# Full attention of a four-block model: maxima as pairs of 64-row products, and the values' products one step later

## The chip, the cores and the metric

The kernel runs on one core of a Trainium2 chip. The metric is the device time of one execution in microseconds (us); of several executions the median is given. The engines are named as the profile names them: PE (TensorE's matrix products) with PEld (its weight loads), DVE (VectorE), ACT (ScalarE), POOL (GpSimd) and SP (SyncE, which here issues the DMAs).

## The reference

The model takes x of 4 batches, 1024 places and 128 channels through four blocks, each x + s * silu(f), with s an attention-like layer and f a feed-forward-like one. The change is in the attention of the third block (number 2), with 16 heads of 8 channels and no mask:

```python
x_norm = layer_norm(x, g1, beta1)
q = (x_norm @ Wq + bq).reshape(B, S, H, hd).transpose(0, 2, 1, 3)
k = (x_norm @ Wk + bk).reshape(B, S, H, hd).transpose(0, 2, 1, 3)
v = (x_norm @ Wv + bv).reshape(B, S, H, hd).transpose(0, 2, 1, 3)
q = apply_rope(q)
k = apply_rope(k)
q = q * (1.0 / jnp.sqrt(jnp.float32(hd)))
scores = jnp.einsum('bhqd,bhkd->bhqk', q, k)
attn = jax.nn.softmax(scores, axis=-1)
out = jnp.einsum('bhqk,bhkd->bhqd', attn, v)
```

Everything is float32. Blocks 0 and 1 have attentions of the same size with a window of 250 places and with a causal mask; the same function of the kernel, `_attention`, does all three, with `mode` "window", "causal" or "full".

## The kernel before

**Products of parts.** Scores are wanted in float32 precision from bfloat16 products. `_split` cuts q and k into three bfloat16 parts each, whose sum is the float32 number. A head has 8 channels, so all nine products of a part of q with a part of k fit into one product with 72 rows of contraction: tile `q9` holds in rows 24r to 24r+23 the three parts of q, for r = 0, 1, 2, and `k9` holds in the same rows the r-th part of k three times. Rows 72 to 74 of `k9` are ones; there `q9` takes the negative maximum of each query's scores, again in three parts, so that the score product itself subtracts the maximum. The rows above are zero against one.

**Units.** A unit is one batch and a group of four heads; there are 16 (`order`). For each:

- `load(n)` (L278) fills a pair `q9`, `k9` from DRAM with three DMAs for q and nine for k, and one that clears rows 72 to 74 of `q9` where an earlier unit left maxima. There are three pairs, used in turn.
- `maxima(n)` (L293) makes 32 steps. A step (`tile_of`) makes the scores of 128 queries of one head against all 1024 keys: two products into the two banks of a `max_ps` tile (PSUM, two such tiles), then one DVE reduction (L344) to the negative maximum. Two ending steps: `split` cuts the maxima into parts on POOL, `spread` turns them with PE and writes them with three DMAs (L371) into rows 72 to 74 of `q9`.
- `attend(n)` (L397) goes through 16 blocks (two halves of 512 queries, eight tiles of 128 keys). In a block, `weights` makes for each of the four heads the scores of 128 keys against 512 queries (tile `sc`, one of three PSUM banks) and their exponential on ACT (L417) into `pt`, a tile for two heads out of five buffers; `values` multiplies the weights with the values, the four heads side by side in four tiles of 32 columns of the array, and adds up over the eight blocks of a half in `o_ps`. Those products are float32 (two records each in the profile).

**Order.** The order on PE is the order of the program (`keep_in_program_order`); on the other engines and SP a scheduler orders what is ready. `rest` (L524) runs for each unit n the list `ahead` (20 steps of the maxima of unit n+1, `split`, then 12 steps of unit n+2 with `spread` of unit n+1 among the last) against the list `weights`, one step of each in turn (`_interleave`). In `weights` each block has two steps: `first` makes the scores of heads 0 and 1, `second` the values of the block before (`lag` is 1 for "full") and then the scores of heads 2 and 3. So PE's order in a block is: maxima, scores, maxima, values, scores. Other layers' steps are spread over the units as further lists (`plan`): the projections of the next batch, the second block's router and experts, a feed-forward layer, whose hidden tiles `h2` come from the five `pt` buffers too, and the ends of the block. Before the first unit, `begin` projects batch 0, issues `load(0)` and `load(1)` and makes all maxima of unit 0 and 12 steps of unit 1, among the products of the first router's experts. `load(n+2)` is issued at the start of unit n.

The line in `attend` that the change moves:

```python
            def second(hn=hn, i=i):
                if i >= lag:
                    values(*blks[i - lag])
                pair.pop(hn)(1)
```

Of the kernel before, what the change touches and what calls it, by code (L numbers as in the profile page):

```python
# [22 lines left out]
F32 = mybir.dt.float32  # L23
BF16 = mybir.dt.bfloat16
AF = mybir.ActivationFunctionType
ALU = mybir.AluOpType
AX = mybir.AxisListType
PSUM = bass.MemoryType.PSUM

P = 128  # L30
B, T, C = 4, 1024, 128
NT = T // P
# [57 lines left out]
def _ps1(k, name, shape=(P, 512), dtype=F32):  # L90

    return k.ps.tile(list(shape), dtype, tag="s", name=name, bufs=3)


def _ps2(k, name):

    return k.ps.tile([P, 2, 512], F32, tag="m", name=name, bufs=2)
# [88 lines left out]
def _attention(k, pool, mode, xT, w, out, rope=None):  # L186
# [7 lines left out]

    nc = k.nc
    scale = HD**-0.5
    dense = {}
    units = {}  # L200
    place = 16 * ("window", "causal", "full").index(mode)

    ps1, ps2 = (lambda name: _ps1(k, name)), (lambda name: _ps2(k, name))
    matmul, transpose = (lambda *args, **kw: _mm(k, *args, **kw)), (lambda *args: _tr(k, *args))
# [73 lines left out]
    def load(n):  # L278

        b, g = order[n]  # L280
        q9, k9 = k.q9[(place + n) % 3], k.k9[(place + n) % 3]
        heads = slice(4 * g, 4 * g + 4)
        for r in range(3):
            rows = slice(24 * r, 24 * r + 24)
            nc.sync.dma_start(q9[rows], dense["q", b][:, heads, :])
            of = dense["k", b][8 * r : 8 * r + 8, heads, :].unsqueeze(0).to_broadcast([3, 8, 4, T])
            for s in range(3):
                nc.sync.dma_start(k9[24 * r + 8 * s : 24 * r + 8 * s + 8], of[s])
        if place + n > 2:
            nc.sync.dma_start(q9[72:75].rearrange("p h t -> p (h t)"), k.zeros)  # L290
        units[n] = (q9, k9)

    def maxima(n):  # L293

        held = {}

        def tile_of(parts):


            def step():  # L300
                q9, k9 = units[n]
                if "neg" not in held:
                    held["neg"] = pool.tile([P, 4, NT], F32, tag="neg", name="neg", bufs=3)
                neg = held["neg"]
                ps = ps2("max_ps")
                flat = ps.rearrange("p a c -> p (a c)")
                _, qt0, _ = parts[0]
                lo = max(0, qt0 - 2) * P if mode == "window" else 0
                hi = T if mode == "full" else (qt0 + 1) * P
                width = hi - lo  # L310
                for j, qt, place in parts:
                    lhs = q9[:, j, qt * P : qt * P + P]
                    for c0 in range(lo, hi, 512):
                        c1 = min(c0 + 512, hi)
                        at = place + c0 - lo
                        masked = mode != "full" and c1 == hi
                        matmul(
                            flat[:, at : at + c1 - c0],
                            lhsT=lhs,
                            rhs=k9[:, j, c0:c1],  # L320
                            start=True,
                            stop=not masked,
                            skip_group_check=True,
                        )
                        if masked:
                            mw = min(c1 - c0, k.mask[mode].shape[1])

                            W = k.mask[mode].shape[1]
                            spans = [(W - P, W)]
                            if W - mw < W - CONTEXT:  # L330
                                spans.insert(0, (W - mw, W - CONTEXT))
                            for m0, m1 in spans:
                                matmul(
                                    flat[:, at + c1 - c0 - W + m0 : at + c1 - c0 - W + m1],
                                    lhsT=k.ident16,
                                    rhs=k.mask[mode][:, m0:m1],
                                    start=False,
                                    stop=m1 == W,
                                    skip_group_check=True,
                                )  # L340
                j0, m = parts[0][0], len(parts)
                stride = parts[1][2] - parts[0][2] if m > 1 else width
                of = flat[:, 0 : m * stride].rearrange("p (n c) -> p n c", n=m)[:, :, 0:width]
                nc.vector.tensor_reduce(neg[:, j0 : j0 + m, qt0], of, AX.X, ALU.max, negate=True)  # L344

            return step

        steps = []
        for qt in range(NT):
            width = T if mode == "full" else min((qt + 1) * P, 3 * P if mode == "window" else T)  # L350

            pitch = 128 if width == 128 else 256 if width == 256 else 512 if width <= 512 else 1024
            per = min(4, 1024 // pitch)
            for j in range(0, 4, per):
                steps.append(tile_of([(j + i, qt, i * pitch) for i in range(per)]))

        def split():
            neg = held.pop("neg")
            held["p"] = parts = pool.tile([P, 3, 4 * NT], BF16, tag="negp", name="negp", bufs=2)
            tmp = pool.tile([P, 4 * NT], F32, tag="negt", name="negt", bufs=2)  # L360
            _split(nc, nc.gpsimd, neg.rearrange("p j t -> p (j t)"), parts, tmp)

        def spread():
            q9, parts = units[n][0], held.pop("p")
            tp = _ps1(k, "neg_ps", (12 * NT, P), BF16)
            transpose(tp, parts.rearrange("p s c -> p (s c)"), k.ident16)
            rows = pool.tile([12 * NT, P], BF16, tag="negr", name="negr", bufs=2)
            nc.vector.tensor_copy(rows, tp)
            for s in range(3):
                to = q9[72 + s : 73 + s].rearrange("o j (t q) -> o (j t) q", t=NT)  # L370
                nc.sync.dma_start(to, rows[4 * NT * s : 4 * NT * s + 4 * NT, :])  # L371

        return steps, [split, spread]


    blocks = [[], []]
    lag = 1 if mode == "full" else 2
    for hf in range(2):
        for kt in range(NT):
            c0 = max(512 * hf, 0 if mode == "full" else kt * P)  # L380
            c1 = min(512 * hf + 512, (kt + 3) * P if mode == "window" else T)
# [15 lines left out]
    def attend(n):  # L397
        b, g = order[n]
        q9, k9 = units.pop(n)
        va = dense["va", b]  # L400
        held = {}
# [66 lines left out]
        blks = [(hf, i) for hf in range(2) for i in range(len(blocks[hf]))]  # L468
        steps = []
        pair = {}  # L470
        for i, hn in enumerate(blks):

            def first(hn=hn):
                pair[hn] = weights(*hn)
                pair[hn](0)

            def second(hn=hn, i=i):
                if i >= lag:
                    values(*blks[i - lag])
                pair.pop(hn)(1)  # L480
                if i > lag and blks[i - lag - 1][0] < blks[i - lag][0]:
                    normalize(0)

            steps += [first, second]
# [31 lines left out]
    order = [(b, g) for b in range(B) for g in range(4)]  # L516
    N = len(order)
    steps, ending = maxima(0)
    begin = project(0) + [lambda: load(0), lambda: load(1)] + steps + ending
    steps, ending = maxima(1)  # L520
    lead = 2 * len(steps) // 5
    begin += steps[:lead]
# [1 line left out]
    def rest(plan):  # L524

        nonlocal steps, ending
        late = []
        for n, (b, g) in enumerate(order):
            ahead = []
            if n + 1 < N:  # L530

                ahead = steps[lead:] + ending[:1]
                last = ending[1]
                if n + 2 < N:
                    load(n + 2)
                    steps, ending = maxima(n + 2)
                    ahead += steps[: lead - 2] + [last] + steps[lead - 2 : lead]
                else:
                    ahead.append(last)
            weights, closing = attend(n)  # L540
            streams = [ahead, weights]
            if b + 1 < B and g < 3:
                if g == 0:
                    coming = project(b + 1)
                streams.append((coming[:3], coming[3:7], coming[7:])[g])
            if late:

                for i in range(lag + 1):
                    weights.insert(1 + 2 * i, late[i])
                for i, step in enumerate(late[lag + 1 :]):  # L550
                    weights.insert(min(len(weights), 2 * lag + 4 + 3 * i), step)
            _interleave(*streams, *plan.get(n, []))
            late = closing + (finish(b) if g == 3 else [])
        _run(late)
# [1490 lines left out]
```

## Time and profile before

| What | Time or share |
|---|---|
| median of three runs (lowest, highest) | 3613.82 us (3608.35, 3614.92) |
| the profiled execution; its span | 3610.66 us; 3608.9 us |
| busy share of the span: PE, DVE, ACT, POOL | 87%, 68%, 55%, 39% |
| third attention: first load, last `sc` product | 1391 us, 2491 us |
| maxima of all three attentions: products; reductions | 625.0 us busy; 1177.9 us busy |
| exponentials of all three attentions | 1077.9 us busy |
| granted TensorE clock, mean over the span | 0.951 |

Busy time of an engine is the time in which at least one of its instructions runs. Matmuls overlap, so their lengths in the profile are longer than what each adds; the distance of two starts is what counts. A line of a wait names who waited, for whom, the total in us, how often, and the longest. An idle engine costs only if something on the path to the end waits for it.

### The profile page before, as it was taken

The numbers are of one execution on the slowest core, as the hardware profiler recorded it, in microseconds if no ns is written. First come the engines' busy times: TensorE is split into PE (matmuls) and PEld (weight loads), VectorE is DVE, ScalarE is ACT, GpSimd is POOL, SyncE is SP. The second block draws the span as 40 slices with busy tenths as digits, with TensorE's granted clock in tenths as the row PEclk, the third lists the DMA queues.
The fourth block names the chain that finished last, engine by engine and source line by source line (L and its number), as shares of the span: only waits on it lengthen the run. The fifth ranks groups of instructions, "written<-read, shape, count | busy, mean of one in ns | idle before, by whom it ended". The sixth has DMA issues, their size and how long they took to land. (4 is left out here: it accounts for less than half of the span.)

```text
span 3608.9 us, 64740 instructions
## 1 busy us (share of the span) xinstructions
PE 3138.7 (87%) x24592; PEld 1704.4 (47%) x24729; DVE 2445.6 (68%) x4927; ACT 1988.7 (55%) x4191; POOL 1417.2 (39%) x1962
## 2 busy tenths in 40 slices
PE   4889889999898986899999989677499999989897
PEld 3545446654343433433323333223366666666665
DVE  7667664457777752788786766652587888778785
ACT  2444453346555552366665665554366666666674
POOL 5555552012323223030321300211576667656663
PEclk8999999999999997999999999888699999999999
DMA  3322312112222102011111221100210111010110
GB/s 99 71 60 55 70 42 83 46 33 51 57 42 57 34 22 69 21 44 28 41 34 33 55 53 31 33 19 9 78 22 18 21 25 24 18 25 22 29 26 21
DMA packets 133083, 146.09 MB, mean 40 GB/s; under 512 B 80403, under 2 KB 107931, under 8 KB 125467
## 3 DMA queue, kind: packets, MB, share of 16 engines
q1 hardware_dynamic: 130724, 137.75, 16.0%
q0 software_dynamic: 2048, 4.20, 0.4%
q8 instruction: 196, 3.21, 0.4%
q14 instruction: 115, 0.93, 0.1%
HBM read 93.83 MB, written 30.11 MB: 34 GB/s over the span
## 5 line engine op out<-in xcount | busy, mean ns | idle before, releaser
L417 ACT ACTIVATE pt<-sc 128x512 f32<-128x512 f32 (+3 forms) x2432 | 1077.0, 511 | 786.1 <-PE sc L78 737.7
L344 DVE TENSOR_REDUCE neg<-max_ps 128x1 f32<-128x1024 f32 (+6 forms) x1088 | 1177.9, 1102 | 477.2 <-PE max_ps L78 424.1
L78 PE MATMUL sc<-q,k 128*128 128x512 bf16 (+3 forms) x2403 | 651.8, 342 | 126.2 <-ACT pt L417 70.0
L78 PE MATMUL max_ps<-k,q 128*128 128x512 bf16 (+3 forms) x2198 | 625.0, 350 | 86.2 <-DVE neg L344 39.5
L78 PE MATMUL o_ps<-pt,va 128*32 128x512 f32 (+3 forms) x4864 | 560.6, 527 | 19.9 <-POOL pt L387 10.2
L387 POOL TENSOR_SCALAR_AFFINE_SELECT pt<-pt 128x256 f32<-128x256 f32 (+2 forms) x768 | 292.3, 399 | 568.2 <-ACT pt L417 566.3
L78 PEld LDWEIGHTS <-k 128*128 128x128 bf16 x2432 | 183.0, 98 | 544.2 <-issue 418.1
L78 PEld LDWEIGHTS <-q 128*128 128x128 bf16 x2304 | 222.7, 99 | 359.6 <-issue 241.2
L168 POOL CAST negp<-neg 128x32 bf16<-128x32 f32 x48 | 10.2, 212 | 719.3 <-DVE neg L344 719.2
L1603 ACT ACTIVATE pr<-lsc,nb,r 128x128 f32<-128x128 f32 x512 | 202.7, 476 | 61.2 <-DVE nb L1595 57.6
L1524 POOL TENSOR_TENSOR qn<-qn,rot 128x512 f32<-128x512 f32 x128 | 164.9, 1294 | 139.8 <-DVE rot L1516 125.9
L1533 POOL TENSOR_TENSOR rn<-ss,neghalf 128x16 f32<-128x16 f32 x64 | 188.9, 2951 | 68.8 <-DVE ss L1531 59.3
L78 PEld LDWEIGHTS o_ps<-pt,va 128*32 128x32 f32 x4864 | 99.7, 109 | 213.8 <-issue 160.3
L691 ACT ACTIVATE h<-hp,eb 128x512 f32<-128x512 f32 x128 | 80.9, 684 | 197.8 <-PE hp L78 190.2
L78 PEld LDWEIGHTS <-ident 128*128 128x128 bf16 x1472 | 146.2, 100 | 87.5 <-issue 22.7
L1441 PE MATMUL qk_ps<-wqkv,hT 128*128 128x512 f32 x256 | 137.9, 623 | 24.9 <-DVE hT L1487 10.3
L78 PE MATMUL hp<-xT,ew 128*128 128x512 f32 x256 | 130.3, 634 | 19.7 <-ACT rope_t L234 9.3
L701 DVE SCALAR_TENSOR_TENSOR xn<-op,gates,xn 128x128 f32<-128x128 f32 x256 | 72.1, 344 | 100.4 <-PE op L78 100.4
L78 PEld LDWEIGHTS op<-ew,h 128*128 128x128 f32 x1024 | 123.6, 192 | 20.1 <-issue 17.0
L78 PE MATMUL max_ps<-mask_window,ident 128*128 128x134 bf16 (+2 forms) x960 | 132.0, 221 | 0.0
L78 PE MATMUL op<-ew,h 128*128 128x128 f32 x1024 | 125.3, 276 | 0.0
L65 POOL TENSOR_TENSOR ln_rs<-ln_ve,neghalf 128x4 f32<-128x4 f32 x72 | 73.7, 1025 | 113.1 <-DVE ln_ve L63 109.7
(347 smaller groups left out, 5452.9 us busy)
## 6 DMA issues: line engine op xcount, KB each, us to landing
q<-qx SPq DMA_DIRECT2D x144, 192.0 KB
k<-kx SPq DMA_DIRECT2D x432, 64.0 KB
va<-vb SPq DMA_DIRECT2D x120, 128.0 KB
x<-x SPq DMA_DIRECT2D x20, 512.0 KB
qx<-qp SPq DMA_DIRECT2D x12, 768.0 KB
kx<-kp SPq DMA_DIRECT2D x12, 768.0 KB
ew<-in_e1w_dram SPq DMA_DIRECT2D x64, 128.0 KB
x<-in_x_dram SPq DMA_DIRECT2D x8, 512.0 KB
```

What stands on the lines that cost most here:

```text
L65: nc.gpsimd.tensor_tensor(rs, ve, k.neghalf[:, :n], ALU.pow)
L78: k.tc.keep_in_program_order(k.nc.tensor.matmul(*args, **kw))
L168: eng.tensor_copy(dst[:, 0], src)
L344: nc.vector.tensor_reduce(neg[:, j0 : j0 + m, qt0], of, AX.X, ALU.max, negate=True)
L387: nc.gpsimd.affine_select(out=pt, in_=pt, pattern=[[0, 2], [step, pt.shape[2]]], compare_op=ALU.is_ge, fill=0.0, base=base, channel_multip ...
L417: nc.scalar.activation(pt[:, j % 2, :width], sc[:, :width], AF.Exp, scale=scale)
L691: nc.scalar.activation(h[:, hh, :], hp[:, hh, :], AF.Gelu, bias=eb1[:, e, hh : hh + 1])
L701: nc.vector.scalar_tensor_tensor(to, op[:, c, :], gates[:, 4 * n + c, e : e + 1], to, ALU.mult, ALU.add)
L1441: pin(nc.tensor.matmul(*args, **kw))
L1524: nc.gpsimd.tensor_tensor(qn[:, i], qn[:, i], rot, ALU.add)
L1533: nc.gpsimd.tensor_tensor(rn, ss.rearrange("p w h -> p (w h)"), k.neghalf[:, : 2 * NH], ALU.pow)
L1603: nc.scalar.activation(t.pr[:, h, :], t.sc[r][:, c, :], AF.Exp, bias=t.nb[r][:, c : c + 1], scale=t.r8[:, h : h + 1])
```

## The change

Only `mode == "full"` changes.

- **Pairs of heads in 64 rows.** The third pair of tiles `q9`, `k9` is cut into two halves, and `load_pairs(n)` fills a half `q8`, `k8`: rows 0 to 63 hold two heads, rows 64 to 127 two others, each with eight of the nine products of parts (the product of the two smallest parts is left out of the maxima). That takes 22 DMAs. `pair` makes for one tile of queries, half of the keys and head i the product in rows 0 to 63 and that of head i+2 in rows 64 to 127, into the two banks of a `max_ps` tile; one reduction gives two maxima, of half the keys each. `split` takes the smaller of the two halves' negative maxima first. It is 32 steps a unit, as before.
- **Loads.** `load(n)` uses two pairs of tiles in turn and clears nothing. At the start of unit n it is `load(n + 1)` and `load_pairs(n + 2)` that are issued; at the start of the stage `load_pairs(0)`, `load(0)`, `load_pairs(1)`.
- **Values.** In `second` the values of the block before come after the scores of heads 2 and 3.

```diff
     def load(n):
         b, g = order[n]
-        q9, k9 = k.q9[(place + n) % 3], k.k9[(place + n) % 3]
+        i = n % 2 if mode == "full" else (place + n) % 3
+        q9, k9 = k.q9[i], k.k9[i]
...
-        if place + n > 2:
+        if mode != "full" and place + n > 2:
             nc.sync.dma_start(q9[72:75].rearrange("p h t -> p (h t)"), k.zeros)
         units[n] = (q9, k9)

+    def load_pairs(n):
+        b, g = order[n]
+        q8, k8 = (t_[2][:, 2 * (n % 2) : 2 * (n % 2) + 2, :] for t_ in (k.q9, k.k9))
+        for a in range(2):
+            heads = slice(4 * g + 2 * a, 4 * g + 2 * a + 2)
+            for r in range(3):
+                r0, ns = 64 * a + 24 * r, 3 if r < 2 else 2
+                nc.sync.dma_start(q8[r0 : r0 + 8 * ns], dense["q", b][0 : 8 * ns, heads, :])
+                for s in range(ns):
+                    nc.sync.dma_start(k8[r0 + 8 * s : r0 + 8 * s + 8], dense["k", b][8 * r : 8 * r + 8, heads, :])
+        pairs[n] = q8, k8
...
+        def pair(part, qt, i):
+            def step():
+                q8, k8 = pairs[n]
+                if "neg" not in held:
+                    held["neg"] = pool.tile([P, 2, 4, NT], F32, tag="neg", name="neg", bufs=3)
+                ps = ps2("max_ps")
+                for a in range(2):
+                    rows = slice(64 * a, 64 * a + 64)
+                    matmul(
+                        ps[:, a, :],
+                        lhsT=q8[rows, i, qt * P : qt * P + P],
+                        rhs=k8[rows, i, 512 * part : 512 * part + 512],
+                        start=True,
+                        stop=True,
+                    )
+                nc.vector.tensor_reduce(held["neg"][:, part, i::2, qt], ps, AX.X, ALU.max, negate=True)
+            return step
...
+        if mode == "full":
+            steps = [pair(part, qt, i) for qt in range(NT) for part in range(2) for i in range(2)]
...
         def split():
             neg = held.pop("neg")
+            if mode == "full":
+                nc.vector.tensor_tensor(neg[:, 0], neg[:, 0], neg[:, 1], ALU.min)
+                neg = neg[:, 0]
...
             def second(hn=hn, i=i):
-                if i >= lag:
+                if i >= lag and mode != "full":
                     values(*blks[i - lag])
                 pair.pop(hn)(1)
+                if i >= lag and mode == "full":
+                    values(*blks[i - lag])
...
+    if mode == "full":
+        loads = [lambda: load_pairs(0), lambda: load(0), lambda: load_pairs(1)]
+    else:
+        loads = [lambda: load(0), lambda: load(1)]
+    begin = project(0) + loads + steps + ending
...
+                if mode == "full":
+                    load(n + 1)
                 if n + 2 < N:
-                    load(n + 2)
+                    (load_pairs if mode == "full" else load)(n + 2)
```

## The prediction

> **What bounds the kernel now.** The page shows three blocks of the model after one another; the change touches the third attention, which runs from about 1390 to 2495 us. I first took the busy time of each engine over the part in which attention and maxima run together, and over one unit (batch, group of four heads) with little else in it. Columns: window, its length, busy us (instructions) of PE, PEld, DVE, ACT, POOL, then granted clock, DMA share, GB/s.
>
> ```profile
> 1490.00:2432.50 942.50, 831.52 (x4492) 300.15 (x4576) 677.53 (x875) 578.28 (x1073) 197.13 (x204) 0.97 0.15 35
> 1677.30:1727.50 50.20, 47.77 (x264) 15.14 (x267) 44.37 (x59) 33.28 (x64) 1.39 (x4) 1.00 0.13 25
> ```
>
> PE is busy for 88% and 95%; DVE (72%, 88%) is next. What PE waits for in the same 942 us is little:
>
> ```profile
> PE sc L78 <- ACT pt L417: 32.5, 39, 7.2
> PE max_ps L78 <- DVE neg L344: 29.7, 22, 14.1
> PE sc L78 <- DVE at L461: 16.6, 1, 16.6
> ```
>
> That is about 90 us of 942 with small ones, so elsewhere PE's own order sets the pace. One block of it, in order of time (start, length, engine, line, tile, rows*columns, moving operand, number):
>
> ```profile
> 1645.69 1.06 PE L78 MATMUL o_ps<-pt,va 128*32 128x512 f32 x8
> 1646.69 0.61 PE L78 MATMUL sc<-q,k 128*128 128x512 bf16 x2
> 1647.14 0.59 PE L78 MATMUL max_ps<-k,q 128*128 128x512 bf16 x2
> 1647.57 0.64 PE L78 MATMUL sc<-q,k 128*128 128x512 bf16 x2
> 1648.05 0.59 PE L78 MATMUL max_ps<-k,q 128*128 128x512 bf16 x2
> 1648.57 0.64 PE L78 MATMUL o_ps<-pt,va 128*32 128x512 f32 x4
> ```
>
> Read the starts, not the lengths, which hold latencies that overlap. A block takes 2.88 us: values 1.00, scores 0.45, maxima 0.43, scores 0.48 (0.05 of it waits for ACT to free the third score bank), maxima 0.52. A pair of maxima products steps by 0.43, so one streams in 0.215. The second of the last pair starts at 1648.26 in the single records and would be done at 1648.475, but the values' weights only load at 1648.57: **0.09 us are lost where the array goes from whole to 32-column tiles**. Leaving them costs the same: the second wave of values starts 0.453 after the first at 1645.695, lasts 0.427, and the next load is at 1646.689, 0.094 late.
>
> Does going to 64 rows cost this too? The trace has such places in the last block of the model:
>
> ```profile
> 2710.75 0.59 PE L1441 MATMUL lsc<-mask_local,ident 128*128 128x512 bf16 x2
> 2711.27 0.33 PE L1441 MATMUL lsc<-qkT 64*64 64x64 f32 x6
> ```
>
> Two whole-array products at 0.215 end at 2711.18; the tiles start at 2711.27: 0.09 again. Out of 64*128 (`y_ps<-state,cT`) single records give the same.
>
> **The change, part by part.**
>
> *Maxima.* A tile of 128 queries against 1024 keys is two whole-array products now, 0.43 us. It becomes two products of 64 rows and 512 keys, for heads i and i+2, in two banks. If they run side by side the pair takes 0.011 (weights: a first score matmul after a switch lasts 390 ns, a later one 379) + 0.215 + 0.007 (the step between side-by-side starts in the values) and 0.094 for leaving: 0.325. Between two whole-array neighbours it causes two switches, so 0.43 goes but 0.325 and a switch into it (0.094, counted with the scores before it) come: hardly a gain. The gain lies where maxima stand beside the values, as values to maxima is one switch in place of one.
>
> *Order of a block.* Now: values, scores, maxima, scores, maxima; two switches. After: maxima, scores, maxima, scores, values; all five borders switch. The block of after: maxima 2 x 0.325 = 0.650; first scores 0.444 + 0.094 = 0.538; second scores 0.444 + 0.092 + 0.043 (the fourth score needs the first exponential to be done, which it is 1.137 after the first score's load) = 0.579; values 0.994 with their exit. Sum 2.761 against 0.994 + 0.447 + 0.431 + 0.478 + 0.522 = 2.872: **0.111 us less per block**.
>
> *How many.* Of 16 x 32 tiles, 44 (unit 0 and twelve of unit 1) run before the first attention unit, between whole-array products of the experts: 2 x 0.105 more and 0.208 less, nothing. The other 468 make 234 blocks: 234 x 0.111 = **26.0 us**.
>
> *What takes some of it back.* (a) Projections, expert and feed-forward products that fall between values and maxima make one switch into two; two or three a unit, 15 units, 0.105 each: 4 us. (b) Weights tiles (`pt`, 5 buffers) are held longer: the old order has three at its peak, the new one four, since the values of the block before free theirs only after all four scores. The feed-forward layer's `h2` takes up to two from the same five; then the third and fourth exponentials wait for the values to end, and I get about 0.2 us a block for some 15 blocks: 3 us (bounds 0 and 10). (c) Where PE waits anyway, 90 of 942 us, time saved is idle: 9%, 2.4 us.
>
> *DVE.* The reduction reads the same 1024 elements, into two outputs instead of one; in the second attention forms with one and with two outputs both take 1.22 us, so 0. Added: a minimum over 128x32 per unit, not in the trace; between 0.25 (reciprocal, 128x16) and 0.285 (product, 128x128): 16 x 0.27 = 4.3 us on an engine that is 72% busy, beside PE; all of it if that cover went. POOL's split waits for it, but POOL sits idle 468 us there.
>
> *DMAs.* A unit issued 12 loads and one zero fill; now 12 loads, for the next unit and not the one after, and 22 half-size ones for the pairs. SP's queue at the start of a unit:
>
> ```profile
> 1677.27 1.77 SPq L371 DMA_DIRECT2D q<-negr  x3
> 1680.64 0.30 SPq L285 DMA_DIRECT2D q<-qx  x1
> 1680.98 0.97 SPq L288 DMA_DIRECT2D k<-kx  x3
> ...
> 1684.63 0.29 SPq L285 DMA_DIRECT2D q<-qx  x1
> 1685.41 1.84 SPq L288 DMA_DIRECT2D k<-kx  x3
> 1688.72 0.23 SPq L290 DMA_DIRECT2D q<-zeros  x1
> ```
>
> The first waits for the last scores of the unit before, as it did (26.9 us in 13 times). Then 13 issues take 8.3 us, because each waits for the one eight before it to land. Behind them now stand 22 more, then expert weights, stores of projections, and the three writes of the maxima that the next unit's scores need, late in the unit. POOL's queue issues what it did. By bytes (1.18 MB to 2.20 MB) the queue takes 15.5 us, by number (0.64 each) 21.8; I take 18, plus 3.4 to its start and 4 to land: the pairs are there 25 us into the unit. Their first use is step 21 of some 36, 29 us into a 50 us unit. Cost 0, bounds 0 and the rival below. At the stage's start the first tile waits 19.2 us for keys; 16 pieces of 32 KB replace 9 of 64 KB: between 3 less and 3 more, taken as 0.
>
> **Sum**: 26.0 - 4 - 3 - 2.4 = 16.6, say 17 us. The profiled execution took 3610.66 (span 3608.9): 3593.7. The median of the three runs is 3613.82, 3.2 above it: **3597**.
>
> **Two rules weighed.** The values run four tiles in 453 ns against 427 for one, nearly free. The Trainium skill, "TensorE: Matmul & The Clock Gate", Measured speedup vs the span model, gives 3.07 times for four row tiles of 512 columns, 77% of ideal, and speaks against the change: at 77% a pair would take 0.28 and not 0.222, 0.116 more per block, and by the page the whole gain would be gone (an estimate). No row here is that case; the row tiles of `lsc` are shorter.
> The nearest row for a 64-row weight load is fp32 and costs 0.104 (480 against 376 ns); the nearest bf16 one, of 128 rows, costs 0.011, and I take it by type and width. The same page, Weight-path perf modes, lets fast weight load depend on 128 weights that aren't FP32; no run here shows it for 64 rows.
>
> **Rivals.**
> 1. *No net change* (0.16): PE gets its 0.1 but something else takes over. For: DVE's 44.4 of 50.2 us in a light unit; two reductions are 2.44 of a 2.76 block, so 5 us of other DVE work per unit fill it. Against: reductions run back to back at 1.18, and a light unit of 50.2 - 1.8 still leaves 4 us. About 3612.
> 2. *Slow weight load, so slower* (0.09): in 64-row tiles the loads cost 0.104 as in fp32: 0.093 x 2 x 234 = 44 us more, **3641**. It decides from 0.036 a tile up (17 us over 468). Not side by side at all would be 0.208 x 468 = 97 us more, 3694; the 64-row tiles of `lsc` speak against it: records step by 7 ns there.
> 3. *Loads late* (0.10): if the queue keeps the pace of its second half (1684.63 to 1688.72, five issues, 0.82 each), 34 take 28 us, the pairs land at 35 us, 6 after their use, in some eight short units: 48 us, **3645**. It decides from 0.64 per issue. PE would stand at maxima in its order with the scores behind it.
> 4. *More gain* (0.08): values no longer stand before the last two scores, so a late ACT (table loads of 1.28 us) hurts less; if most of the 32.5 us behind ACT goes: 3570.
>
> Forecast 0.57. A measurement here can't tell less than 0.2% (7.2 us) from nothing: faster is below 3606.6, slower above 3621.0. The forecast's own range is 3584 to 3611; 0.05 of it lies within 0.2%, 0.02 above. With rivals: faster 0.50 + 0.08 + 0.02 = 0.60, same 0.05 + 0.13 = 0.18, slower 0.02 + 0.01 + 0.19 = 0.22. The range reaches from rival 4 past rival 1, 3570 to 3626, and leaves out rivals 2 and 3.
>
> **What would show it.** A steady block at 2.76 us, pairs of `max_ps` as 64*128 starting some 7 ns apart, and 0.09 gaps on all five sides; max_ps busy on PE halved. Wrong, if second products start 0.2 later, if gaps around the tiles are 0.2, if PE waits for `k<-kx` or `q<-qx` in mid-unit, if waits behind `pt` grow above 10 us, or if PE falls below 80% with DVE above 90%.

## The result and the profile after

The changed kernel takes 3611.43 us (median, 3605.62 to 3621.36); the kernel before, run beside it, 3612.16 (3605.15 to 3621.34). The ratio is 1.0000 [0.9988, 1.0011]: **no change**, where 3597, 0.5% less, was forecast. The profiled execution has a span of 3609.2 us against 3608.9.

The same window of the attention stage as in the prediction, in the kernel after (columns as there):

```profile
1490.00:2432.50 942.50, 812.02 (x4575) 238.15 (x4573) 678.14 (x890) 576.83 (x1071) 196.26 (x204) 0.95 0.21 52
```

PE is busy for 19.5 us less (831.52 before, where the trace lacks some 80 of as many products, so at least that), its granted clock is 0.95 where it was 0.97, and DMAs move 52 GB/s where they moved 35. What PE waits for in it (who, for whom, total us, times, longest):

```profile
PE sc L78 <- ACT pt L461: 57.4, 32, 34.0
PE max_ps L78 <- DVE neg L332: 40.1, 28, 18.1
...
PE tr_ps L82 <- DMA slots_tm<-sent: 3.8, 1, 3.8
```

Scores behind ACT went from 32.5 to 57.4 us with a single wait of 34.0, maxima behind DVE from 29.7 to 40.1 with one of 18.1, and one wait for a DMA is new. The wait of 16.6 for DVE's `at` is gone. One block of a light unit, in order of time:

```profile
1642.57 0.39 PE L78 MATMUL max_ps<-k,q 64*128 64x512 bf16 x2
1642.89 0.60 PE L78 MATMUL sc<-q,k 128*128 128x512 bf16 x2
1643.42 0.39 PE L78 MATMUL max_ps<-k,q 64*128 64x512 bf16 x2
1643.75 0.60 PE L78 MATMUL sc<-q,k 128*128 128x512 bf16 x2
1644.28 1.07 PE L78 MATMUL o_ps<-pt,va 128*32 128x512 f32 x8
1645.28 0.39 PE L78 MATMUL max_ps<-k,q 64*128 64x512 bf16 x2
```

The two products of a pair run side by side: a pair and the switch out of it take 0.32 to 0.33 us from start to start (0.325 predicted). A block takes 1645.28 - 1642.57 = **2.71 us** (the next one 2.72), some 0.16 less than the 2.872 of before; the prediction had 2.761 and 0.111 less. So PE does in its steady blocks what was forecast, and more. Where this gain is lost again can be read from the lengths of the units. The table is worked out from the starts of the exponentials: a unit lasts from its first exponential to the next unit's first, the last one to its own last; "begin" is from the last exponential of the causal attention to the first of the full one (one execution each, us). The lower rows belong to the experiments.

| kernel | begin | units 0-8 | 9 | 10-11 | 12 | 13 | 14-15 | all units | ratio to before |
|---|---|---|---|---|---|---|---|---|---|
| before | 154.7 | 509.9 | 60.8 | 143.4 | 76.7 | 77.6 | 106.6 | 975.0 | 1 |
| after | 155.3 | 496.5 | 67.9 | 140.8 | 79.3 | 84.0 | 105.2 | 973.6 | 1.0000 |
| e1 | 154.8 | 506.4 | 62.1 | 141.9 | 79.5 | 80.0 | 109.6 | 979.5 | 1.0019 |
| e2 | 158.5 | 499.1 | 67.6 | 136.9 | 82.5 | 82.7 | 105.5 | 974.4 | 1.0025 |
| e3 | 158.7 | 496.7 | 67.9 | 140.8 | 74.1 | 61.0 | 120.5 | 960.9 | 0.9968 |
| e4 | 158.7 | 498.6 | 61.4 | 167.6 | 66.6 | 61.6 | 123.7 | 979.5 | 1.0049 |
| e5 (before + pin) | 150.9 | 510.4 | 62.0 | 140.5 | 68.3 | 64.3 | 120.1 | 965.6 | 0.9962 |
| e6 | 158.4 | 496.6 | 57.7 | 140.8 | 74.1 | 61.0 | 120.4 | 950.5 | 0.9941 |
| e7 | 166.0 | 492.0 | 68.8 | 138.2 | 67.7 | 60.5 | 119.6 | 946.6 | 0.9928 |
| e8 | 155.4 | 499.0 | 67.7 | 136.9 | 74.0 | 61.8 | 123.2 | 962.6 | 0.9969 |
| e9 | 154.3 | 496.8 | 58.2 | 140.8 | 73.8 | 61.0 | 120.5 | 951.1 | 0.9930 |
| e10 | 155.5 | 503.0 | 57.7 | 140.8 | 74.0 | 61.1 | 120.5 | 957.0 | 0.9948 |
| e11 | 163.6 | 490.8 | 56.2 | 136.7 | 68.1 | 60.6 | 120.1 | 932.4 | 0.9902 |
| e12 | 157.5 | 493.2 | 56.2 | 135.1 | 63.8 | 60.2 | 116.9 | 925.3 | **0.9854** |
| e13 (before + pin) | 159.7 | 525.4 | 76.8 | 139.0 | 68.8 | 62.5 | 119.8 | 992.3 | 1.0063 |

Units 0 to 8 give 13.4 us, units 10 and 11 2.6, units 14 and 15 1.4. Unit 9 takes 7.1 back, unit 12 2.6, unit 13 6.4. The two large ones have visible causes. In **unit 9** this is SP's queue after (start, length, queue, tile, number):

```profile
2023.66 1.44 SPq L308 DMA_DIRECT2D k<-kx  x2
2025.30 0.93 SPq L1115 DMA_DIRECT2D slots_tm<-sent  x2
```

and before, in the same place of the program:

```profile
2017.75 0.93 SPq L1063 DMA_DIRECT2D slots_tm<-sent  x2
...
2025.43 0.32 SPq L285 DMA_DIRECT2D q<-qx  x1
```

Before, the read of the second block's expert rows (`slots_tm`) was issued ahead of the unit's loads, 8.6 us ahead of the unit's first exponential (at 2026.30); after, it is the last of a run of loads, 11.9 us behind it (2013.40). PE turns these rows in its fixed order and stands, with everything behind it (PE's line in the kernel after):

```profile
2028.37 0.74 PE L82 MATMUL tr_ps<-ident,slots_tm 128*128 128x128 f32 x5 [3.76 <-DMA slots_tm<-sent]
...
2031.69 1.71 PE L78 MATMUL o_ps<-pt,va 128*32 128x512 f32 x8
```

The values behind this wait take 1.64 us to the start of the next product (2033.33), where they take 1.00 in the block above: PE runs more slowly for a while. A second wait of 3.66 us, behind DVE (2.22 in the same unit before), is followed by the same.

In **unit 13** ACT of the kernel after shows, among its exponentials,

```profile
2327.78 1.08 ACT L461 ACTIVATE pt<-sc 128x512 f32<-128x512 f32 x2 [0.33 <-PE sc L78]
...
2334.44 1.06 ACT L705 ACTIVATE xn<-xn 128x1024 f32<-128x1024 f32 x1 [0.72 <-POOL xn L87]
2361.75 1.06 ACT L705 ACTIVATE xn<-xn 128x1024 f32<-128x1024 f32 x1 [26.25 <-POOL xn L87]
```

The silu of a batch of the second block's output stands there right behind the one of another batch and waits 26.25 us for POOL; no exponential passes it in that time, and PE's scores wait 34.0 us for a free bank. Before, eight exponentials stood between the two:

```profile
2340.34 1.06 ACT L653 ACTIVATE xn<-xn 128x1024 f32<-128x1024 f32 x1 [0.72 <-POOL xn L87]
...
2342.71 1.08 ACT L417 ACTIVATE pt<-sc 128x512 f32<-128x512 f32 x2
2355.27 1.09 ACT L417 ACTIVATE pt<-sc 128x512 f32<-128x512 f32 x2 [11.48 <-PE sc L78]
2358.96 1.09 ACT L417 ACTIVATE pt<-sc 128x512 f32<-128x512 f32 x2 [2.60 <-PE sc L78]
2360.61 1.09 ACT L417 ACTIVATE pt<-sc 128x512 f32<-128x512 f32 x2 [0.56 <-PE sc L78]
...
2367.74 1.06 ACT L653 ACTIVATE xn<-xn 128x1024 f32<-128x1024 f32 x1 [0.72 <-POOL xn L87]
```

PE's order is written in the program; ACT's, DVE's and SP's are made by a scheduler, and for the changed program it made another order.

### The profile page after: what moved, and what is told of

It reads as the page before. It is cut to its first block, busy times and chain, and to the rows that moved or that the text cites. A ratio compares the mean times of both kernels' runs of the same rounds, so it can differ in the third digit from the quotient of the medians.

```text
span 3609.2 us, 65151 instructions
## 1 busy us (share of the span) xinstructions
PE 3120.1 (86%) x24729; PEld 1639.8 (45%) x24729; DVE 2444.0 (68%) x4943; ACT 1986.8 (55%) x4189; POOL 1413.6 (39%) x1962
## 5 line engine op out<-in xcount | busy, mean ns | idle before, releaser
L78 PE MATMUL sc<-q,k 128*128 128x512 bf16 (+3 forms) x2432 | 661.3, 344 | 136.6 <-ACT pt L461 95.9
L332 DVE TENSOR_REDUCE neg<-max_ps 128x2 f32<-128x1024 f32 x512 | 609.9, 1219 | 211.8 <-PE max_ps L78 210.5
L383 DVE TENSOR_REDUCE neg<-max_ps 128x2 f32<-128x768 f32 (+6 forms) x576 | 567.3, 998 | 253.3 <-PE max_ps L78 240.1
L78 PE MATMUL max_ps<-k,q 64*128 64x512 bf16 (+4 forms) x2304 | 540.3, 355 | 91.1 <-DVE neg L332 43.9
L78 PE MATMUL o_ps<-pt,va 128*32 128x512 f32 (+3 forms) x4864 | 558.3, 527 | 16.3 <-POOL pt L431 10.2
L78 PEld LDWEIGHTS <-q 128*128 128x128 bf16 (+1 forms) x2304 | 176.6, 96 | 480.5 <-issue 427.1
L78 PEld LDWEIGHTS <-k 128*128 128x128 bf16 x2432 | 165.9, 98 | 431.0 <-issue 377.4
```

Of the source, the lines that this page charges most:

```text
L78: k.tc.keep_in_program_order(k.nc.tensor.matmul(*args, **kw))
L332: nc.vector.tensor_reduce(held["neg"][:, part, i::2, qt], ps, AX.X, ALU.max, negate=True)
```

## The experiments

Two main theories: the 64-row pairs and the new order of the values do what was forecast, and the loss lies in orders on ACT and SP that the change upset; or the pairs themselves cost elsewhere what they gain here. Letters in the expectations are names of theories. Every ratio is to the kernel before, run beside it.

**Each half alone (e1, e2).** e1 is the kernel before with the values behind the four scores; e2 is the kernel after with the values back ahead of the second scores.

```diff
 # e2; e1 has the other order in the kernel before
-                if i >= lag and mode != "full":
+                if i >= lag:
                     values(*blks[i - lag])
                 pair.pop(hn)(1)
-                if i >= lag and mode == "full":
-                    values(*blks[i - lag])
```

> The kernel before with only the values moved behind the four scores. Theory A (what pays is the pairs of 64-row products, and the order of the values hardly matters while ACT keeps up): a steady block stays at 2.85 to 2.88 us, two changes of the array's shape per block, time within 5 us of before. Theory B (the order is what shortens the block): steady block at 2.75 or less, 20 us faster.

> The changed kernel with the values back ahead of the last two scores. Theory A (five changes of shape in either order): steady block 2.70 to 2.80 us as in the changed kernel (2.72), the time within 5 us of it. Theory B: the values then wait for ACT, block 2.85 or more, 20 us slower than the changed kernel.

e1: 3615.87 us, 1.0019 [1.0010, 1.0029]. e2: 3618.10, 1.0025 [1.0015, 1.0034]. Each is over the 5 us that theory A allowed (e1 6.4 above before; e2's ratio is some 9 us above that of the kernel after), and far from the 20 of theory B. The commonest blocks of units 0 to 8 take 2.87 and 2.83 us in the code of before (e5's trace), 2.83 in e1, 2.76 in e2 and 2.72 in the kernel after, so of the shorter block at most 0.04 are the order's, the rest the pairs'. In units 0 to 8 the values' order gives 3.5 us, the pairs 10.8, both together 13.4. Units 9, 12 and 13 spoil each: unit 9 is long in both kernels with pairs (67.6 in e2, 67.9 in the kernel after; 62.1 in e1), units 12 and 13 in both. Of e1's span 4.4 us lie before the last causal exponential, in code that it doesn't touch, so its loss against before is partly not its own.

**The order on ACT (e3, e5).** The silu of the second block's batches is kept where the program has it (the pin), behind that batch's rows, first in the changed kernel, then in the kernel before.

```diff
-        return [lambda n=n: fetch(n) for n in range(b * NT, b * NT + NT)] + [None, weigh] + _silu_steps(k, [b])
+        def silu():
+            pin(nc.scalar.activation(xn[:, a, :], xn[:, a, :], AF.Silu))
+        return [lambda n=n: fetch(n) for n in range(b * NT, b * NT + NT)] + [None, weigh, silu]
```

> The changed kernel with the three silu of the experts' gates held in program order on ACT. Theory C (some 17 us that the shorter blocks save are given back in units 9, 12 and 13, the largest part where two silu stand back to back on ACT and the first exponential behind them is 34 us late): the 34 us wait of the scores goes, a wait of 10 to 20 us behind DVE may come in its place as in the kernel before, unit 13 falls from 84 to 70 to 78 us, 6 to 14 us faster. Theory D (units 12 and 13 end when the gathers of the experts' rows are done, whatever ACT's order): unit 13 stays at 82 to 85, no change in the time.

> The kernel before with the three silu of the experts' gates held in program order on ACT. Theory C (the place of the silu is an accident of the schedule that costs the changed kernel more than the one before, whose second and third silu stand eight exponentials apart): 0 to 6 us faster than before, so that with the silu held in both the pairs are worth 6 to 12 us. Rival E (holding the silu is worth as much in either, and the pairs nothing): 10 to 13 us faster.

e3: 3597.89 us, 0.9968 [0.9959, 0.9978]. Unit 13 falls from 84.0 to 61.0, and units 14 and 15, where the work goes, grow by 15.3. PE's waits of e3 between 1490 and 2432 us:

```profile
PE max_ps L78 <- DVE neg L332: 40.7, 26, 11.8
PE sc L78 <- ACT pt L461: 23.4, 35, 2.7
```

The wait of 34.0 is gone, the longest behind ACT is 2.7. But e5, the same pin without the change, has 3597.24 us, 0.9962 [0.9947, 0.9976]. The misplaced silu is real and worth 12 to 14 us (0.32 and 0.38%), in *both* kernels: before, it went with the wait of 16.6 for `at`; the longest wait that e5 lists in the same window is 9.4, behind DVE's reductions. So it is not what took the change's gain away; with the pin in both, the pairs are still worth nothing. That theory fell.

**The loads (e4, e6).** e4 issues the nine-row loads of the next unit ten steps into a unit, in every unit; e6 is e3 with this in unit 9 alone.

```diff
-                if mode == "full":
+                if mode == "full" and n == 9:  # e4: for every n
+                    ahead.insert(10, lambda n=n: load(n + 1))
+                elif mode == "full":
                     load(n + 1)
```

> The changed kernel with load(n+1) issued ten steps into unit n, not at its start. Theory C (in unit 9 the experts' rows, slots_tm, stand behind more loads than before on SP's queue, and PE waits for them and then runs at half clock): slots_tm is issued some 5 us sooner, PE's 3.8 us wait for it goes, unit 9 falls from 68 to 60 to 64 us; 4 to 7 us faster. Theory D: unit 9 stays at 66 to 68 us, since the DVE wait of 3.7 us and ACT's work there set it.

> As e3_pin_silu, and load(n+1) ten steps into the unit in unit 9 alone. Theory C (unit 9 loses to the late experts' rows): units 0 to 8 as in e3, unit 9 at 60 to 63 us and not 68, units 10 and 11 as in e3 (65, 76): 5 us faster than e3. Rival D: what unit 9 wins, units 10 to 12 lose, since the loads that come later hold up what comes behind them on SP: the same as e3 or slower.

e4: 3629.38 us, 1.0049 [1.0036, 1.0062]. Unit 9 falls by 6.5 us as expected, but units 10 and 11 grow by 26.8 and 14 and 15 by 18.5, while 12 and 13 shrink by 35.1: the scheduler arranges the rest anew. A change of order in every unit is not one change. e6: 3592.02 us, 0.9941 [0.9924, 0.9958]; unit 9 takes 57.7 us for e3's 67.9, every other unit is within 0.2 of e3's. In SP's queue of e6 the experts' rows stand ahead of the nine-row loads (`q<-qx` here is the first of them), 0.3 us ahead of the unit's first exponential (at 2019.01; in e3 they come 11.9 behind it):

```profile
2018.68 0.93 SPq L1117 DMA_DIRECT2D slots_tm<-sent  x2
2019.71 0.37 SPq L252 DMA_DIRECT2D qx<-qp  x1
2020.18 0.40 SPq L289 DMA_DIRECT2D q<-qx  x1
```

PE's `tr_ps` then shows no wait, the wait behind DVE falls from 3.71 to 0.78 and the unit's granted clock is 1.00 (0.95 in the kernel after). The 12 issues of `load(n + 1)` in front of a foreign read cost unit 9 its 10.2 us. Against e5, the pairs now gain 15.1 us over all units, though unit 12 is 5.8 longer; the begin takes back 7.5.

**The begin (e9, e10).** From the reduction of the first maxima tile to the first full exponential kernels with pairs need 102 to 105 us, those without 94.5 to 98 (the first one comes some 3 us sooner with pairs). e9 is e6 with the maxima of units 0 and 1 in the old form; e10 is e6 with the same tiles, and most of the begin's loads issued between them.

```diff
 # e9
-        if mode == "full":
+        if mode == "full" and n > 1:
             steps = [pair(part, qt, i) for qt in range(NT) for part in range(2) for i in range(2)]
...
-        loads = [lambda: load_pairs(0), lambda: load(0), lambda: load_pairs(1)]
+        loads = [lambda: load(0), lambda: load(1)]
 # e10
-        loads = [lambda: load_pairs(0), lambda: load(0), lambda: load_pairs(1)]
+        loads = [lambda: load_pairs(0)]
...
+        steps[28:28] = [lambda: load_pairs(1)]
+        steps[16:16] = [lambda: load(0)]
```

> The kernel with silu pinned and unit 9's loads ten steps later, with the maxima tiles of the first two units (44 of them lie among the expert products ahead of the attention, the other 20 in unit 0) put back into the old form: one head by 1024 keys over the whole array, from the nine-row tiles, with 26 load issues in place of 56. Theory F (pairs cost the begin): from last causal exponential to first full exponential 158.4 us there; back to 151 plus or minus 2 as in the kernel before with the pin, and unit 0 1 to 2 us longer, so 4 to 7 us off the whole: ratio 0.9922 to 0.9930 against 0.9941. Rival G (the begin is long because the causal attention ends sooner there and the experts' weights come at their own time): begin stays at 156 or more, time the same or 1 us worse.

> The same kernel with pairs everywhere, only the loads of the begin moved: unit 0's nine-row tiles issued after 16 of its 32 maxima tiles, unit 1's paired rows after 28, where all 56 issues stood ahead of the first maxima tile. If the begin's loss is the 34 extra load issues (their bytes crowding the expert weights, the granted clock 0.81 in the first half): begin 152 to 154, total 4 to 6 us less than 3592. If it is the tiles' changes of shape between whole-array expert products and the PSUM pairs' wait on DVE: begin stays at 157 to 159 and the total within 1.5 us of 3592.

The first half of the begin in e6, then in e5 (columns as above):

```profile
1418.60:1470.00 51.40, 41.27 (x184) 22.53 (x184) 31.73 (x47) 8.86 (x14) 0.00 (x0) 0.85 0.30 63
```

```profile
1418.00:1466.00 48.00, 38.06 (x186) 22.89 (x185) 33.71 (x48) 8.87 (x14) 0.00 (x0) 0.96 0.22 48
```

With pairs the same work has more load traffic beside it (share 0.30 against 0.22) and a lower granted clock (0.85 against 0.96; the first half of the kernel before has 0.24 and 0.91). e9: begin 154.3 and 97.9 from first tile to exponential, as in the kernel before, and unit 0 1.9 longer; time 3590.61, 0.9930 [0.9917, 0.9944], which can't be told from e6's 0.9941. So the pairs seem to cost the begin some 4 us, and the old form gives nearly half of that up again in unit 0. (4 is the difference of means: 153.5 over before, e1 and e5, from 150.9 to 154.8 with the same code there, and 157.5 over after, e2, e3, e4, e6 and e8, from 155.3 to 158.7. Between before and after themselves it is 0.6.) e10: the begin falls by 2.9 us, to 155.5, as long as in the kernel after with all loads ahead; unit 0 grows by 7.0 (53.3 to 60.3), 6.6 of it a wait of PE behind DVE's reductions and none behind a load; 3595.44, 0.9948 [0.9936, 0.9961]. Neither theory came, and how the loss divides between loads and changes of shape stays open.

**Fewer changes of shape (e7, e8, e11, e12).** e7 takes two tiles together ahead of a block's first scores and the values ahead of the second scores (tiles, scores, values, scores: four changes a block and not five), with the pin; e8 is its control, e3 with that order of the values. e11 adds e6's late loads in unit 9 to e7, e12 also e9's old form of the first two units.

```diff
 # e7 (and the order of e2, the pin of e3)
-            steps = [pair(part, qt, i) for qt in range(NT) for part in range(2) for i in range(2)]
+            steps = [
+                lambda two=(pair(part, qt, 0), pair(part, qt, 1)): [one() for one in two]
+                for qt in range(NT) for part in range(2)
+            ]
+            for step in steps:
+                step.tiles = True
...
+            first.opens = True
...
+                for step in weights:
+                    if getattr(step, "opens", False):
+                        while ahead:
+                            merged.append(ahead.pop(0))
+                            if getattr(merged[-1], "tiles", False):
+                                break
+                    merged.append(step)
+                streams[:2] = [merged + ahead]
```

> Maxima of two tiles together ahead of the first two scores of a block, the values again between the pairs of scores, silu held as in e3. Four changes of shape a block instead of five and 0.09 less: theory A (what changes of shape cost is what counts on PE): steady block 2.62 (0.55 + 0.54 + 0.99 + 0.54), 240 fewer changes, some 10 us faster than e3. Rival F (DVE, with 2.36 us of reductions per block, is the bound by then, or two tiles together wait for its banks): steady block 2.70 or more with waits of max_ps behind neg over 60 us in the stage, no faster than e3.

> As e3_pin_silu, with the values ahead of the last two scores as before the change. Theory A (order of no matter): within 4 us of e3. Rival B (the order is worth what e1 and e2 hint at, 5 us either way): 5 to 9 us slower than e3.

> Two tiles together ahead of a block's first scores (silu pinned, old order of the values) with the nine-row loads of unit 10 issued six steps into unit 9. Unit 9 took 68.8 us with two tiles and 57.7 in the other kernel once its loads stood behind the experts' rows. Theory (the experts' rows wait behind 19 load issues on SP's queue): unit 9 falls by 8 to 11 us, the stage to 936 to 939, and the whole to 3577 to 3582, ratio 0.990 to 0.9915. Rival (with the tiles bunched the unit is long by its own waits): unit 9 stays above 64 and the time above 3585. The begin stays at 116 us from first tile to first exponential, as nothing is changed there.

> Two tiles together, silu pinned, unit 9's loads later, and the first two units' maxima in the old form as in e9_begin_whole (unit 1's two tiles at a time). Theory: bunched pairs cost the begin 163.6 us (109.0 from first tile to first exponential, 42 changes of shape, 46.8 us in waits over 0.25 us), whole-array tiles 154.4; the begin falls by 8 to 10, unit 0 grows by 1 to 2, so the whole by 6 to 9 us to 3570 to 3573, ratio 0.988 to 0.9885. Rival: the bunching, not the form of the tile, costs the begin (the experts' own products wait for two DVE maxima at a time): begin stays at 160 or more and the whole within 2 us of 3579. Unit 12, which the pairs lengthened by 5.8 us with the pin (68.3 to 74.1) and two tiles together did not (68.1), stays at 68 in both.

e7: 3587.95 us, 0.9928 [0.9912, 0.9944]; e8: 3599.41, 0.9969 [0.9955, 0.9983], as e3: the order of the values alone is worth nothing here. e7's block is 2.61 to 2.63 us as expected, though its begin is 7.3 longer than e3's. e11: 3579.18, 0.9902 [0.9887, 0.9918]: unit 9 falls from 68.8 to 56.2, as expected. e12: 3558.46 us, **0.9854 [0.9838, 0.9870]**, faster than any other. Its begin is 6.1 us shorter than e11's, where 8 to 10 were expected; units 10 to 12 and 14 to 15 are 9.1 shorter besides, and the part behind the last exponential, in code that no edit touches, 4.1. The theory didn't say this, and nothing here explains it. A block of e12:

```profile
1642.86 1.06 PE L78 MATMUL o_ps<-pt,va 128*32 128x512 f32 x8
1643.86 0.61 PE L78 MATMUL sc<-q,k 128*128 128x512 bf16 x2
1644.39 0.60 PE L78 MATMUL max_ps<-k,q 64*128 64x512 bf16 x4
1644.93 0.61 PE L78 MATMUL sc<-q,k 128*128 128x512 bf16 x2
1645.47 1.07 PE L78 MATMUL o_ps<-pt,va 128*32 128x512 f32 x8
```

It takes 2.61 us: one change of shape less than the 2.71 of the kernel after.

**Is it the pairs or the grouping (e13)?** The kernel before with the pin and with whole-array tiles two at a time.

> The kernel before with silu pinned and whole-array maxima taken two at a time ahead of a block's first scores, no pairs: what e12 has except the pairs and their loads. Theory P (the 64-row pairs make e12's gain, grouping only lets them): no change of shape is saved here, 2 a block as before, so units 1 to 8 stay at 54 to 58 us (450 to 455 us in all; e12 437) and the time within 0.3% of the kernel before with the pin: ratio 0.993 to 0.999. Rival Q (the grouping alone makes the gain, since DVE and PE wait less for each other): units 1 to 8 at 440 or less, ratio below 0.99.

3630.75 us, 1.0063 [1.0049, 1.0077], slower than both theories said. Unit 5 takes 68.7 us where e5 has 56.7, for one wait:

```profile
1812.83 1.09 PE L82 MATMUL ot<-ident,os 128*128 128x128 f32 x4 [18.96 <-DVE os L453]
```

Unit 9 has another of 18.9. Without unit 5, units 0 to 8 take 456.7 us; e5 453.7; e12 438.2. Its begin is 8.8 longer than e5's. So grouping without pairs shortens nothing and brings two new waits behind DVE's copy of the sums. With pairs it pays; in units 0 to 8 the gain needs both. Of the rest of e12's margin over e5 a part is not shown to be theirs: in the profiled executions units 0 to 8 give 17.2 us and the later units 23.1, the begin takes 6.6, and 7.7 more lie behind the last exponential.

## Why the prediction was wrong

- **"A steady block at 2.76 us"**: right in kind, too small. It is 2.71, because the 0.043 us counted for the fourth score's wait for a bank isn't there. The changes of shape cost what was read before: single records give 0.093 to 0.101 us on all five sides. (Two sums are loosely written: 0.011 + 0.215 + 0.007 + 0.094 is 0.327, and the 0.094 behind the values counts from the last of the four tiles, which starts 0.020 after the first.) From first to last full exponential the records hold 511 changes before and 1255 after. At 0.094 each that is 70 us more, against some 95 less streaming (468 tiles at 0.43 before and 0.322 - 0.094 after; both are estimates from these figures). PE's own work thus fell by about what the sum says.
- **234 x 0.111 = 26.0**: units 0 to 8, 144 blocks of these, should have given 16.0 less their part of (a), 2.4: 13.6. They gave 13.4. That the two agree is partly luck. At the measured 0.16 a block they should have given 23; only 62 of the 144 blocks have the steady length. The changes of shape beyond three a block are 25 there, 2.4 us, as (a) has it. PE's waits over 0.15 us grew by 0.9. The granted clock, for which the prediction has no term, fell by 0.03 in units 2, 3 and 5, which is up to 4.8 us (an estimate: 0.03 of their 159 us). Unit 3, in which most of the prediction's light window lies, did not shrink at all (50.6 to 51.2 us).
- **(c), "where PE waits anyway, time saved is idle: 9%, 2.4 us"**: this step failed. The waits were taken as a fixed length. They are places in orders that a scheduler makes: PE's idle gaps over 0.25 us between first and last full exponential rose from 98.0 to 121.4 us, 23.4 where 2.4 were counted. Unit 13 lost 6.4 us by the silu's new place. e3 and e5 show how large such a place is (23.0 us of unit 13 in one, 13.3 in the other), and also that the kernel before paid for the same silu, so that with the pin in both it no longer tells them apart.
- **"DMAs. Cost 0"**: this step failed too. The working asked when the pairs' own rows land; those were never waited for, though the last of the 34 issues came 29 us into a light unit. It named expert weights, stores and the writes of the maxima as standing behind the new issues and priced none of it; the experts' rows it didn't name. The read of these in unit 9 cost 7.1 us, shown by e6 (10.2 us back).
- **The 44 tiles of the begin, "nothing"**: 0.6 us between before and after, some 4 on the mean of the runs; with whole tiles there (e9) the begin is as before, at 1.9 in unit 0.
- **(a)** fits: 1255 changes are 744 more than before, 42 beyond the three for each of 234 blocks, 4 us. **(b)** came, near its size, in units 7, 11 and 15, where the feed-forward layer's products are: ACT's exponentials wait for the values in six places there and in none before. e1 has these waits too, e2 has but one of 0.7 in unit 7; unit 7 takes 65.7 us after and 63.9 in e2. In the whole stage such waits of ACT grew from 2.7 to 7.4 us.
- **DVE 0** holds for the reduction: it takes 1.22 us as before, and two fit into 2.71.
- **Rivals.** 1, no net change, is what came, mainly by another mechanism: DVE at 88% was not the new bound, since e12 runs the same reductions in less time, though PE's waits behind reductions in units 0 to 8 grew from 10.2 to 14.0 us. 2 fell: the pairs step at 0.32 to 0.33 with their switch. 3 came near, in another place: late were not the pairs' keys but rows behind them. 4 didn't come: waits behind ACT grew, from 32.5 to 57.4 us, which the prediction had named as a sign of being wrong.

With the pin in both kernels (e5 against e6 and e9) the pairs are worth 0.2 to 0.3% (e6's interval overlaps that of e5, e9's lies just below it); grouped, 1.1% (0.9854 against 0.9962), with the reserve said at e13. Unit 12 is 5.8 us longer in e3 and e6 than in e5; PE's waits in it are 18.2 us in e6 and 15.3 in e5, its granted clock 0.84 and 0.93. What order on the other engines makes this was not found, nor why e12's late units are shorter than e11's.

The Trainium skill, "TensorEngine Tiling (Array Packing)", Key Properties, says that a change of the tiling mode drains the TensorE. The trace agrees in that PE's next product comes late at every such change, and gives the size that page leaves out: 0.093 to 0.101 us, the same from whole to 32 columns as into 64 rows.

## What to carry to other kernels

Where one engine's order is fixed and the others' is made by a scheduler, a gain in steady blocks is only kept if the orders around it stay: compare the length of every unit, and look at the long single waits before the steady state is judged. Price what stands *behind* a queue's new issues, not only what they bring. Where a sum agrees for a part of the run, count that part with the measured prices too, before the agreement is taken as proof. When a change of the array's shape has a price, bundle what has the same shape; leaving tiles whole where their neighbours are whole paid only with bundled tiles here (e12 against e11), and with single ones no difference showed (e9 against e6).

## What the runs showed of the hardware

- The change of shape costs the same 0.09 to 0.10 us between whole array, 32 columns and 64 rows in this stage, also for bf16 tiles of 64 rows; a 64-row weight load in bf16 is not slow (a pair's matmuls last 372 to 387 ns, a whole-array one 376 to 379).
- Two 64-row products of 512 columns run side by side almost for the price of one: a pair with its switch steps by 0.32 to 0.33 us, of which 0.09 to 0.10 is the switch; one whole-array product streams in 0.215.
- The granted clock was lower in units in which PE had long single waits, so that a wait went with a loss above its length: unit 13 has 0.78 after and 0.85 before, unit 9 has 0.95 after and 1.00 in e6. 0.05 of 67.9 us is 3.4 us (an estimate from these rows); the wait in front of `tr_ps` was 3.76, another behind DVE 3.66 (0.78 in e6), and the unit lost 10.2. The Trainium skill, "TensorE: Matmul & The Clock Gate", Part 1, has the clock halved after an idle window of about 3.4 us; the waits of 3.76 and 3.66 us agree with that order of size. No threshold can be read here: unit 2 after has 0.94 with no wait above 2.79 us, unit 9 before 1.00 with one of 2.22, and no run varied the length alone.
